# Loading x of seven of the 32 tiles in transfers of 120, 7 and 1 rows

## The chip, the cores and the metric

The kernel runs on one core of one Trainium2 chip. The metric is the device time of one execution in microseconds (us), taken as the median of several runs; each time comes from the chip itself. A profile of one execution, with the start and duration of every instruction and of every DMA packet, stands beside the times.

## The reference

The input x has 4096 rows of 32 fields with 64 numbers each; W has one 64x64 matrix for each of the 496 pairs of fields (i < j). For every row and pair, field i is multiplied by the pair's matrix, and the product is multiplied element by element by field j:

```python
vi = inputs[:, i_idx, :]                       # (B, 496, 64)
vj = inputs[:, j_idx, :]
vdotw = jnp.einsum('bpd,pde->bpe', vi, W)
inter = vdotw * vj
return inter.reshape(B, -1)                    # (4096, 31744), float32
```

x is 33.6 MB, W some 8 MB, the output 520 MB: nearly all that moves is the output.

## The kernel before

The 4096 rows are cut into 32 tiles t = 0..31 of 128 rows, one row to a partition. For each tile the kernel transposes x (TensorE, L130, two halves of eight 128x128 blocks, each copied out of PSUM by ScalarE at L131), multiplies by W (TensorE, L170), multiplies the result in PSUM by field j (VectorE, L180 and L188, written to the buffer `ring`), and stores `ring` to the output.

**Stores.** The 16 pairs of fields of a tile are grouped by `STORES` into four groups of 7552, 6528, 7872 and 9792 columns. Each group is stored by one DMA on SyncE's queue (L194), 128 rows of 30208, 26112, 31488 or 39168 bytes. `ring` has 28160 columns, fewer than the 31744 of one tile: a group's place is taken in turn, and starts again at 0 where the group no longer fits. VectorE may write a place only when the store that last read it has landed, so about three groups are on their way at a time. A DMA of 128 rows runs on all 16 DMA engines, 8 rows to each, and it has landed when the last of the 16 is done.

**Loads of x.** `xbuf` has three places for a tile of x, 2048 columns each. `x_slots` makes the list of loads: tile 0 alone, then two tiles to a load, `[(1,1),(2,2)]`, `[(4,0),(3,1)]`, `[(5,1),(6,2)]`, `[(8,0),(7,1)]` and so on (tile, place), and tile 31 alone. The host lays x out in this order, so that each partition's part of a load is one contiguous piece of DRAM, 16384 bytes for two tiles. `load_x` (L106) issues a load as one DMA on ScalarE's queue:

```python
nc.scalar.dma_start(
    out=xbuf[:, s * F * D : s * F * D + n],
    in_=x[at : at + P * n].rearrange("(p c) -> p c", p=P),
)
```

A load waits until VectorE has done the last product that reads the places it writes. For `[(8,0),(7,1)]` these are the places of tiles 4 and 5, so it goes out when tile 5 is done. The framework has eight semaphores for completions of DMAs and gives them out in turn; an issue also waits until the last DMA that had the semaphore has landed.

**Order on ScalarE's queue.** Between two loads stand four copies L131 (two tiles of two halves). The first half of tile t+1 is transposed at group member `FIRST_HALF_AT` = 9 of tile t, in the last of the four groups; its second half at member `SECOND_HALF_AT` = 3 of tile t+1 itself, in the second group.

**W** is loaded once at the start by five DMAs on SyncE's queue (L142).

Of the kernel before, what the change touches and what calls it, by code (L numbers as in the profile page):

```python
# [1 line left out]

# [6 lines left out]

F32 = mybir.dt.float32  # L10
ALU = mybir.AluOpType

P = 128
BANK = 512
BANKS = 8

STORES = [[0, 1], [2, 3], [4, 5, 6], [7, 8, 9, 10, 11, 12, 13, 14, 15]]

LOADS = [[0], [1], [2, 3], [4, 5, 6], [7, 8, 9, 10, 11, 12, 13, 14, 15]]


FIRST_HALF_AT, SECOND_HALF_AT = 9, 3
RING = 28160


def x_slots(NT):


    loads = [[(0, 0)]]
    for t in range(1, NT, 2):  # L30
        if t + 1 == NT:
            loads.append([(t, 1)])
        elif loads[-1][-1] == (t - 1, 2):
            loads.append([(t + 1, 0), (t, 1)])
        else:
            loads.append([(t, 1), (t + 1, 2)])
    return loads


@with_exitstack  # L40
def pair_bilinear_kernel(
    ctx: ExitStack,
    tc: tile.TileContext,
    x: bass.AP,
    w: bass.AP,
    out: bass.AP,
    F: int,
    D: int,
):

    nc = tc.nc
    NT = out.shape[1] * 2 // (F * (F - 1) * D)
    NPR = F // 2

    width = [(F - 1 - i) * D for i in range(F)]
    off = [sum(width[:i]) for i in range(F)]
    cols = sum(width)  # L80


    woff = [i % 2 * D + sum(width[i % 2 : i : 2]) for i in range(F)]
    store_w = [sum(width[2 * p] + width[2 * p + 1] for p in g) for g in STORES]

    const = ctx.enter_context(tc.tile_pool(name="const", bufs=1))
    psum = ctx.enter_context(tc.tile_pool(name="ps", bufs=1, space=bass.MemoryType.PSUM))

    ident = const.tile([P, P], F32, tag="ident", name="ident")
    make_identity(nc, ident)  # L90

    def runs(tl, a, b, n):

        ap = tl[:, a : a + n]
        return bass.AP(ap.tensor, ap.offset, [list(ap.ap[0]), [b - a, 2], list(ap.ap[1])])

    xbuf = const.tile([P, 3 * F * D], F32, tag="x", name="x")
    x_loads = x_slots(NT)
    slot = {t: xbuf[:, ts(s, F * D)] for load in x_loads for t, s in load}

    def load_x(load):

        at = sum(len(before) for before in x_loads[: x_loads.index(load)]) * P * F * D
        n = len(load) * F * D
        s = load[0][1]
        nc.scalar.dma_start(  # L106
            out=xbuf[:, s * F * D : s * F * D + n],
            in_=x[at : at + P * n].rearrange("(p c) -> p c", p=P),
        )

    pring = psum.tile([P, BANKS * BANK], F32, tag="pring", name="pring")
    bank = 0

    def take_banks(n):

        nonlocal bank
        if bank + n > BANKS:
            bank = 0
        got = pring[:, bank * BANK : (bank + n) * BANK]
        bank = (bank + n) % BANKS  # L120
        return got

    xT = const.tile([P, NPR * P], F32, tag="xT", name="xT")

    def transpose_x(xt, g):

        n = 2 * BANK // P
        pt = take_banks(2)
        for c in range(n):
            nc.tensor.transpose(pt[:, ts(c, P)], xt[:, ts(n * g + c, P)], ident)  # L130
        nc.scalar.copy(xT[:, ts(g, 2 * BANK)], pt)  # L131

    ring = const.tile([P, RING], F32, tag="ring", name="ring")
    at = 0

    load_x(x_loads[0])
    w_sb = const.tile([P, sum(width[0::2])], F32, tag="w", name="w")
    done = 0
    for g in LOADS:

        upto = woff[2 * g[-1]] + width[2 * g[-1]]
        nc.sync.dma_start(out=w_sb[:, done:upto], in_=w[:, done:upto])  # L142
        done = upto

    transpose_x(slot[0], 0)
    for t in range(NT):
        xt = slot[t]
        for load in x_loads:
            if min(load)[0] == t + 1:
                load_x(load)  # L150
        for s, group in enumerate(STORES):
            if at + store_w[s] > RING:
                at = 0
            osb = ring[:, at : at + store_w[s]]
            at += store_w[s]
            o0 = off[2 * group[0]]
            for p in group:
                if p == SECOND_HALF_AT:
                    transpose_x(xt, 1)
                if p == FIRST_HALF_AT and t + 1 < NT:  # L160
                    transpose_x(slot[t + 1], 0)
                first = (width[2 * p] - 1) % BANK + 1
                for c1 in range(first, width[2 * p] + 1, BANK):
                    n = first if c1 == first else BANK
                    c0 = c1 - n
                    odd = width[2 * p + 1] and c1 > D
                    pm = take_banks(2)
                    for h in range(1 + bool(odd)):
                        a = woff[2 * p + h] + c0 - h * D
                        nc.tensor.matmul(  # L170
                            pm[:, h * BANK : h * BANK + n],
                            xT[h * D : (h + 1) * D, ts(p, P)],
                            w_sb[h * D : (h + 1) * D, a : a + n],
                            start=True,
                            stop=True,
                        )
                    xj = xt[:, (2 * p + 1) * D + c0 : (2 * p + 1) * D + c1]
                    o = [off[2 * p + h] - o0 + c0 - h * D for h in range(2)]
                    if odd and (c0 or c1 < width[2 * p]):
                        nc.vector.tensor_tensor(  # L180
                            runs(osb, o[0], o[1], n),
                            runs(pm, 0, BANK, n),
                            bass.AP(xj.tensor, xj.offset, [xj.ap[0], [0, 2], xj.ap[1]]),
                            ALU.mult,
                        )
                    else:
                        for h in range(1 + bool(odd)):
                            nc.vector.tensor_tensor(  # L188
                                osb[:, o[h] + h * D : o[h] + n],
                                pm[:, h * (BANK + D) : h * BANK + n],  # L190
                                xj[:, h * D :],
                                ALU.mult,
                            )
            nc.sync.dma_start(  # L194
                out=out[:, t * cols + o0 : t * cols + o0 + store_w[s]], in_=osb
            )


# [30 lines left out]
```

## Time and profile before

| | |
|---|---|
| median of 6 runs | 1336.81 us (1336.66 to 1337.1) |
| the profiled execution: its own time | 1336.8 us |
| its span, first to last instruction | 1335.0 us |
| PE busy | 1161.0 us (87%) |
| DVE busy | 1182.9 us (89%) |
| ACT busy | 66.1 us (5%) |
| DMA | 562.87 MB, mean 422 GB/s |
| mean granted TensorE clock | 0.964 |

PE is TensorE's matmuls, DVE is VectorE, ACT is ScalarE, SP is SyncE; a name with q behind it is the engine's instruction queue. Busy shares are means over the whole span. "A <- B" in a list of waits says that A stood idle until B. Of the DMA packets the trace has the queue, the start, the duration and the size, but not the engine that moved them: q1 is the queue that SP issues to, q10 that of ACT, q8 and q14 carry instructions. One row of a transfer is one packet, and every engine's share of a DMA ends with a packet of 4 bytes, its step of the completion semaphore. The times of the 16 steps of each semaphore are in the trace too.

### The profile page before, as it was taken

To read this page: it belongs to the slowest core of one execution; us is meant where nothing else is said; L and a number is where in the kernel's file an instruction comes from. 1 tells how busy PE (TensorE), PEld (TensorE's weight loads), DVE (VectorE), ACT (ScalarE), POOL (GpSimd) and SP (SyncE) were. 2 spreads that over 40 slices of the span, in tenths; PEclk is the share of its full clock that TensorE was granted. 3 is DMA by queue.
4 is the path that set the end of the run, shared out by engine and by line. 5 is a ranking of instruction groups with operands and counts; after the bars stand their busy time and mean duration, and the time that the engine had idled before them with its cause. 6 is when DMAs were issued, how large, how long until landed. Compare 5 with 4: busy or idle time off the path is not lost.

```text
span 1335.0 us, 13080 instructions
## 1 busy us (share of the span) xinstructions
PE 1161.0 (87%) x5376; PEld 545.7 (41%) x5376; DVE 1182.9 (89%) x1376; ACT 66.1 (5%) x65; POOL 0.7 (0%) x6
## 2 busy tenths in 40 slices
PE   6998989989898898998989889798998979989893
PEld 3443334443344543443444444344443434353441
DVE  5998989989899898998989899898998989989894
ACT  0000000000000000000000000000000000000000
POOL 0000000000000000000000000000000000000000
PEclk9999999999899899999989999999999999989997
DMA  9999999999999999999999999999999999999998
GB/s 397 433 430 431 432 425 431 417 433 431 412 425 410 420 430 427 425 416 433 405 432 431 420 428 411 432 426 420 429 413 431 426 407 418 429 420 424 428 425 352
DMA packets 21659, 562.87 MB, mean 422 GB/s; under 512 B 2400, under 2 KB 2400, under 8 KB 2656
## 3 DMA queue, kind: packets, MB, share of 16 engines
q1 hardware_dynamic: 19152, 528.49, 92.8%
q10 hardware_dynamic: 2448, 33.56, 5.9%
q8 instruction: 42, 0.69, 0.2%
q14 instruction: 17, 0.14, 0.0%
HBM read 41.94 MB, written 520.09 MB: 421 GB/s over the span
## 4 chain that ended last, share of the span: by engine, by line
DMA 46%; DVE 37%; issue 8%; PE 7%; DVEq 0%; ACT 0%
DMA out_dram<-ring 45%; DVE ring L180 32%; PE pring L170 7%; DVE ring L188 5%; DMA x<-in_x_dram 1%; DVEq L180 0%; PE pring L130 0%; ACT xT L131 0%; DVEq L225 0%
## 5 line engine op out<-in xcount | busy, mean ns | idle before, releaser
L170 PE MATMUL pring<-w,xT 64*128 64x512 f32 (+4 forms) x4864 | 1098.8, 564 | 145.7 <-DVE ring L180 133.8
L180 DVE TENSOR_TENSOR ring<-pring,x 128x1024 f32<-128x1024 f32 (+3 forms) x1056 | 1103.6, 1105 | 133.0 <-DMA out_dram<-ring 103.0
L170 PEld LDWEIGHTS pring<-w,xT 64*128 64x128 f32 x4864 | 490.2, 191 | 711.7 <-DVE ring L180 532.0
L131 ACT COPY xT<-pring 128x1024 f32<-128x1024 f32 x64 | 64.8, 1012 | 1224.0 <-PE pring L130 1224.0
L188 DVE TENSOR_TENSOR ring<-pring,x 128x64 f32<-128x64 f32 (+3 forms) x320 | 97.3, 353 | 1.5 <-DMA out_dram<-ring 0.9
L130 PEld LDWEIGHTS pring<-ident,x 128*128 128x128 f32 x512 | 55.5, 142 | 57.8 <-DVE ring L180 49.1
L130 PE MATMUL pring<-ident,x 128*128 128x128 f32 x512 | 70.8, 282 | 8.7 <-DMA x<-in_x_dram 8.7
L131 ACT ACT_TABLE_LOAD x1 | 1.3, 1283 | 1.7 <-PEq L221 1.7
masks.py:199 POOL TENSOR_SCALAR_AFFINE_SELECT ident<-ident 128x128 f32<-128x128 f32 x1 | 0.3, 292 | 0.1
masks.py:197 POOL MEMSET ident<- 128x128 f32 x1 | 0.2, 204 | 0.3 <-POOLq L221 0.3
L221 POOL MEMSET const-bfloat16-1.0<- 128x1 bf16 x1 | 0.1, 101 | 0.0
L221 POOL MEMSET const-uint8-127<- 128x1 uint8 x1 | 0.1, 101 | 0.0
L221 POOL MEMSET const-float32-0.0<- 128x1 f32 x1 | 0.1, 98 | 0.2 <-issue 0.2
L221 POOL MEMSET const-float32-1.0<- 128x1 f32 x1 | 0.1, 98 | 0.0
## 6 DMA issues: line engine op xcount, KB each, us to landing
out_dram<-ring SPq DMA_DIRECT2D x32, 4896.0 KB, 17.7
out_dram<-ring SPq DMA_DIRECT2D x32, 3936.0 KB, 17.9
out_dram<-ring SPq DMA_DIRECT2D x32, 3776.0 KB, 18.0
out_dram<-ring SPq DMA_DIRECT2D x32, 3264.0 KB, 18.6
x<-in_x_dram ACTq DMA_DIRECT2D x15, 2048.0 KB, 20.4
w<-in_w_dram SPq DMA_DIRECT2D x1, 2592.0 KB, 28.3
x<-in_x_dram ACTq DMA_DIRECT2D x2, 1024.0 KB, 12.8
w<-in_w_dram SPq DMA_DIRECT2D x1, 2016.0 KB, 22.3
```

What stands on the lines that cost most here:

```text
L130: nc.tensor.transpose(pt[:, ts(c, P)], xt[:, ts(n * g + c, P)], ident)
L131: nc.scalar.copy(xT[:, ts(g, 2 * BANK)], pt)
L170: nc.tensor.matmul(pm[:, h * BANK : h * BANK + n], xT[h * D : (h + 1) * D, ts(p, P)], w_sb[h * D : (h + 1) * D, a : a + n], start=True, st ...
L180: nc.vector.tensor_tensor(runs(osb, o[0], o[1], n), runs(pm, 0, BANK, n), bass.AP(xj.tensor, xj.offset, [xj.ap[0], [0, 2], xj.ap[1]]), ALU ...
L188: nc.vector.tensor_tensor(osb[:, o[h] + h * D : o[h] + n], pm[:, h * (BANK + D) : h * BANK + n], xj[:, h * D :], ALU.mult,)
L221: nc = bacc.Bacc("TRN2", target_bir_lowering=False, num_devices=1)
```

## The change

Tiles 4, 8, 12, 16, 20, 24 and 28, each of them the first of the two tiles of its load, are loaded in three transfers by rows: 0 to 119, 120 to 126, and 127. The other tile of such a load (3, 7, ... 27) becomes a transfer of 128 rows of its own. So seven of the 17 loads turn from one DMA into four. All other loads, the layout of x in DRAM, the stores and the arithmetic stay.

```diff
+PART_LOADED = [4, 8, 12, 16, 20, 24, 28]
+ROWS = [slice(0, 120), slice(120, 127), slice(127, 128)]
...
-        nc.scalar.dma_start(
-            out=xbuf[:, s * F * D : s * F * D + n],
-            in_=x[at : at + P * n].rearrange("(p c) -> p c", p=P),
-        )
+        dst = xbuf[:, s * F * D : s * F * D + n]
+        src = x[at : at + P * n].rearrange("(p c) -> p c", p=P)
+        if not any(t in PART_LOADED for t, _ in load):
+            nc.scalar.dma_start(out=dst, in_=src)
+            return
+        for k, (t, _) in enumerate(load):
+            c = ts(k, F * D)
+            for r in ROWS if t in PART_LOADED else [slice(0, P)]:
+                nc.scalar.dma_start(out=dst[r, c], in_=src[r, c])
```

In the changed program the order of the instructions on TensorE, VectorE and SyncE is that of before. On ScalarE's queue the three transfers of tile 8 (and likewise of 4, 12, ...) stand two copies earlier than the load did, since they now need the place of tile 4 alone; the 128 rows of tile 7 stand where the load stood.

## The prediction

> **What bounds the kernel now.** I read the page's busy slices first, then the waits, then the list of DMA issues, and last the trace's packets and semaphore steps.
>
> ```profile
> PE 1161.0 (87%) x5376; PEld 545.7 (41%) x5376; DVE 1182.9 (89%) x1376; ACT 66.1 (5%) x65; POOL 0.7 (0%) x6
> ...
> DMA  9999999999999999999999999999999999999998
> ...
> DMA out_dram<-ring 45%; DVE ring L180 32%; PE pring L170 7%; DVE ring L188 5%; DMA x<-in_x_dram 1%; DVEq L180 0%; PE pring L130 0%; ACT xT L131 0%; DVEq L225 0%
> ```
>
> The 16 DMA engines are at 90% or more nearly throughout, and stores are the largest part of the chain that ended last. The waits say that VectorE is held by stores, not by its own work:
>
> ```profile
> DVE ring L180 <- DMA out_dram<-ring: 103.0, 43, 6.2
> DVE ring L180 <- PE pring L170: 19.0, 10, 13.7
> ```
>
> VectorE needs (1182.9 + 19 + the few us of smaller gaps) / 32, some 38 us a tile; a tile takes 41 (between two x loads, issued at 253.9 and 335.8 us, lie two tiles in 81.9 us). So VectorE has 3 us a tile to spare, and waits for places in `ring`.
>
> A place is free when the slowest of 16 engines is done, and the engines are not alike. The DMA view of the window 1329.9 to 1334 us:
>
> ```profile
> DMA  0000000800000000000000800000000000000000
> ...
> DMA packets 7, 0.08 MB, mean 19 GB/s; under 512 B 5, under 2 KB 5, under 8 KB 5
> ```
>
> Two packets of the last store (2 x 39168 bytes is 0.08 MB) start here, one after the other: one engine works alone until 1333.6, while most ended at 1329.9. Its packets can be followed back, since on one engine each packet starts 4 ns before the last one ends. From about 111 us on the engine that finishes last is always the same unbroken chain. Its 8 rows of the four stores take 9.09, 7.95, 9.61 and 11.88 us (tile 2), those of the others 8.92, 7.72, 9.30 and 11.56: 38.5 against 37.5 us a tile. Two tiles with the x rows (8 x 0.611 = 4.9) make 2 x 38.5 + 4.9 = 81.9 us, just the time between two loads. The slow engine sets the pace. The step of the last engine comes 0.23 us behind the 15th in the first loads, and mostly 1.5 to 4.5 us behind it in the stores after 130 us.
>
> What the other 15 lose by it: fewer than 16 engines have a packet of q1 or q10 under way for 239 engine-us between 60 and 1325 us; 42 stretches of about 0.9, 37 in all, are those where one engine carries a q8 packet, which leaves 202 / 15 = 13.5 us for each. With the end (54.6 / 15 = 3.6) they have 17.1 us to spare.
>
> **The change, part by part.** The profiled run is 1336.8 us, as the median; its last data packet ends at 1333.6. So the run is that end plus 3.2.
>
> *The highest engine.* A tile's 128 rows are 8 to an engine, 8 x 0.611 / 2 = 2.44 us in rows of 16384 bytes. It loses these and gets 1/16 of one row, 512 bytes. That size is not in the trace: it lies between a packet of 4 bytes (9 ns) and one of 7424 (281 ns); 7936 bytes took 300, 16128 took 602, a line through which gives 0.02 to 0.03 us, and I take 0.03. The companion tile's rows become 8192 bytes, 309 ns instead of 305.5: 8 x 3.5 ns, 0.03. Two steps of 9 ns: 0.02. Net -2.36 us, seven times -16.5 (with 281 ns: -14.8).
>
> *Engines 0 to 6.* If 120 rows go 8 each to 15 engines and 7 rows one each to seven, each of the seven gets a row of 309 ns more, and 0.03 + 0.03 + up to 0.04 for the same small parts: +0.41, seven times +2.9. *The others of the 15:* +0.1, +0.7.
>
> *The sum.* Highest engine: 1333.6 - 16.5 = 1317.1, if always busy; at 63 us, where tile 4's part now goes out, each engine has several us of stores queued (first landings come 14.2 us after issue, own work at most 11.6), so a lead of 2.4 us doesn't starve it. Engines 0 to 6: 1329.9 - 13.5 + 2.9 = 1319.3. The latter is more and is the bound. 42 q8 packets fall unevenly (16384 bytes, 0.61 us of work): one or two more than the mean on the worst engine add 0.5 to 1.2. I take 1319.8, and 1319.8 + 3.2 = **1323.0 us**, 13.8 less. Low end: the highest engine's sum, 1320.3, less 3 for slowness that may lessen (below): 1317. High end of this case: a third of the idle time stays, +4.5: 1327.5.
>
> *The issues.* 21 more DMAs on ScalarE's queue at 0.365 us each (median of L106), 7.7 us in all, but three in a row at most. Behind them stands the copy of the next second half; at 335.8 us such a load is issued and the next copy starts at 346.6, so 10 us of idle time cover 1.1. Without that cover TensorE would wait 1.1 us seven times, and VectorE's 3 us a tile would take it. *The semaphores given out in turn:* the new issues wait for DMAs of at least a tile earlier: the single row of tile 8 for the load of 5 and 6, issued a tile before; SyncE's last store of tile 5 for the 120 rows of tile 8, also issued a tile before. A tile is 41 us, and the longest landing is 23.1. Nothing. *The earlier place:* the three parts of tile 8 go out when tile 4 is done, the companion when tile 5 is. The same bytes go through the same queues, in pieces of 2.4 instead of 4.9 us; the store that shares a load's time lands at 22 instead of 17 us, so two smaller delays take the place of one: nothing to half an idle stretch gained.
>
> [...] The rows: 256 packets of 8192 bytes took 309 ns and 1920 of 16384 bytes 611, so halving the piece costs 1% on the engine. [...]
>
> **The rivals.**
>
> *The slow engine isn't the relieved one* (no change). The packets carry no engine's number, so that the chain is the highest engine is not shown. If it is one of 7 to 14, 1333.6 + 0.7 + 3.2 = 1337.5; if one of 0 to 6, 1339.7. For it: nothing in the profile names it. Against it: the extra time that it has to lose, 17.1, is of the size of the relief, which says only that the relief could work. [...] The trace speaks for one slow chain: the second to end does so at 1331.1, only 1.2 us behind the rest.
>
> *The slowness follows whoever trails* (half the gain). The slow chain isn't slow in tiles 0 and 1 (9.30 us for the third store, as all), nor for some 15 us after each x load. Why is not to be read. If being last is what slows, another engine becomes last when this one is relieved. Between nothing and 13.8 I take half, 1330; for it stand the fast early tiles, against it that engines thrown back by a q8 packet (0.4 us and more) go on at full speed.
>
> *The pieces don't spread* (slower). The trace before shows only 128 rows over 16 engines. If 120 rows go to 8 engines, 15 each, these get 7 x 7 x 0.309 = 15.1 us more, and if 7 rows go to one engine, that one 15.1 again: 1329.9 - 13.5 + 30.3 + 0.7 + 3.2 = 1350.6. With the 7 rows alone on one engine it is 1335.4. It decides from 17.1 us more on any one engine; below that there is still a gain. [...]
>
> **How the numbers follow.** A measurement of this kernel tells about 0.2%, 2.7 us, from no change. Forecast (1317 to 1327.5): 0.72. Slowness follows (1327.5 to 1334): 0.11. Not the relieved engine: 0.09, of which 0.05 within 0.2% and 0.04 above it. Pieces don't spread: 0.06, of which 0.02 within 0.2% and 0.04 above. A residue of 0.02 for an unseen wait, slower. So faster 0.83, same 0.07, slower 0.10. The range 1317 to 1333 holds the first two cases, 0.82.
>
> **What would show it.** Right: the two tiles between loads take some 81 us instead of 81.9 on average; VectorE's wait for stores falls from 103 us to below 60; the last step of 16 comes within 2.5 us of the 15th; packets of 512 bytes take 0.02 to 0.05 us, and no engine carries more than 8 rows of a part. Wrong: one chain still trails by 3 us and more in every store (not the relieved engine), rows of 8192 bytes come 15 to an engine (no spread), or waits of ScalarE or SyncE for a DMA appear.

## The result, and the profile after

The changed kernel takes 1340.34 us (median of 15 runs, 1339.89 to 1340.72), the kernel before 1336.85 in the same comparison: slower by 3.5 us, ratio 1.0026 with an interval of 1.0019 to 1.0033. The forecast was 1323.0. The rival "the slow engine isn't the relieved one" gave 1339.7 for a slow engine among 0 to 6.

The page of the changed kernel, queues and span:

```profile
span 1338.4 us, 13133 instructions
...
q1 hardware_dynamic: 19152, 528.49, 92.6%
q10 hardware_dynamic: 3505, 33.56, 5.9%
q8 instruction: 42, 0.69, 0.2%
```

q10 had 2448 packets before. Of the 3505 now, 2048 have 8192 bytes, 1024 have 16384 and 433 are steps of 4 bytes. Of the steps, 17 transfers of 128 rows account for 17 x 16 = 272; the other 161 are 7 x 23, and 23 = 15 + 7 + 1. So 120 rows did go to 15 engines and 7 to seven, but the single row went to one engine as a packet of 8192 bytes; there is no packet of 512.

The waits of VectorE in the changed kernel, beside 103.0 and 19.0 before:

```profile
DVE ring L190 <- DMA out_dram<-ring: 107.3, 44, 6.2
DVE ring L190 <- PE pring L180: 18.1, 8, 13.6
```

The wait for stores was to fall below 60 us; it grew by 4.3. And the end of the changed kernel, its DMA view from 1333.2 to 1338 us:

```profile
DMA  0000007000000000007000000000000000000000
...
DMA packets 6, 0.08 MB, mean 16 GB/s; under 512 B 4, under 2 KB 4, under 8 KB 4
```

This is the picture of before, 3.2 us later: two rows of the last store, one after the other, on one engine alone (to 1336.8; before, to 1333.6). One chain of packets, each starting as the last one ends, still trails the others. Its cycle can be read in the packets as the time between the ends of the second stores of tiles 0, 4, 8 ... 28. These seven periods are longer than before by 0.36 to 0.71 us, 0.46 on average and 3.2 in all: each has one part-loaded tile in it, and one row of 8192 bytes is 0.31 us. So the slow engine seems not to have been relieved but to have got a row more; the runs below test this.

### The profile page after: what moved, and what is told of

Its sections match the earlier page's. It is cut to its first block, busy times and chain, and to the rows that moved or that the text cites. A ratio compares the mean times of both kernels' runs of the same rounds, so it can differ in the third digit from the quotient of the medians.

```text
span 1338.4 us, 13133 instructions
## 1 busy us (share of the span) xinstructions
PE 1159.4 (87%) x5376; PEld 542.6 (41%) x5376; DVE 1182.4 (88%) x1376; ACT 66.1 (5%) x65; POOL 0.7 (0%) x6
## 3 DMA queue, kind: packets, MB, share of 16 engines
q10 hardware_dynamic: 3505, 33.56, 5.9%
## 4 chain that ended last, share of the span: by engine, by line
DMA 47%; DVE 37%; issue 9%; PE 5%; DVEq 0%; ACT 0%
DMA out_dram<-ring 46%; DVE ring L190 32%; DVE ring L198 6%; PE pring L180 5%; DMA x<-in_x_dram 1%; DVEq L190 0%; PE pring L140 0%; ACT xT L141 0%; DVEq L235 0%; DVEq L198 0%
```

## The experiments

Theory A: one fixed engine, among the low-numbered ones, is slow, and its own bytes set the time. Theory B: whoever trails is slowed. Theory C: the order and the issues of the new transfers cost, not the shares of the engines. The median of the kernel before was 1336.9 us in every comparison.

**The split alone, with all shares equal** (e1). Against the changed kernel:

```diff
-ROWS = [slice(0, 120), slice(120, 127), slice(127, 128)]
+ROWS = [slice(0, 128)]
```

> Seven loads are cut into two transfers of 128 rows, one a tile, with the early place of the change, but every engine keeps its 8 rows of each tile. Fixed slow engine among the low-numbered ones (theory A): the extra row of the change is gone, only shorter rows and steps remain, 1337.0 to 1337.6 us. Whoever trails is slowed (theory B): the same, 1337. Cost of order and issues, not of shares (theory C): as the change, 1340.

1337.47 us (1337.36 to 1337.57). The early place, the shorter rows and the seven extra issues cost 0.6 us. Theory C expected 1340 here and falls; the other 2.9 us come with the cut into 120, 7 and 1 rows, that is with the shares and with two more transfers a tile (e3 tells these apart).

**A code by engine** (e2). The last 8 rows are cut differently in the seven tiles:

```diff
-ROWS = [slice(0, 120), slice(120, 127), slice(127, 128)]
+CUT = {4: 127, 8: 127, 12: 126, 16: 126, 20: 125, 24: 125, 28: 124}
...
-            for r in ROWS if t in PART_LOADED else [slice(0, P)]:
+            for r in [slice(0, 120), slice(120, CUT[t]), slice(CUT[t], P)] if t in PART_LOADED else [slice(0, P)]:
```

> As the change with three transfers a tile, but the last 8 rows are cut 7+1, 7+1, 6+2, 6+2, 5+3, 5+3 and 4+4 over the seven tiles, so that engines 0 to 7 get 14, 12, 10, 8, 6, 4, 2 and 0 rows more than with 120 rows (if a transfer of n rows under 16 goes one each to the n lowest engines), each 0.309 us. Theory A: the time above the kernel of e1 tells the number of the slow engine: engine 0 +4.3, 1 +3.7, 2 +3.1, 3 +2.5, 4 +1.9, 5 +1.2, 6 +0.6. Theory B: the engine with most sets it, +4.3. Theory C: 1340, as the change.

1340.21 us, 2.74 over e1. By the expected sums that would be engine 3 (2.5) or 2 (3.1). The periods of the slow chain tell it tile by tile; over those of e1 they are longer by

| last 8 rows cut | 7+1 | 7+1 | 6+2 | 6+2 | 5+3 | 5+3 | 4+4 |
|---|---|---|---|---|---|---|---|
| us more than e1 | 0.49 | 0.50 | 0.40 | 0.58 | 0.32 | 0.31 | 0.04 |

So the slow engine has a row in the transfers of 7, 6 and 5 rows and none in those of 4, 3, 2 or 1: if n rows go to the n lowest engines, it is number 4, the fifth. (This is what "engine 4" means from here on, and "engines 0 to 3" are the four that come before it in this count; no packet shows a number.) Its six rows are 1.9 us; 0.5 more comes with the third transfer of a tile, as the next run shows, and some 0.4 isn't accounted for.

**Two transfers of 4 rows** (e3).

```diff
-ROWS = [slice(0, 120), slice(120, 127), slice(127, 128)]
+ROWS = [slice(0, 120), slice(120, 124), slice(124, 128)]
```

> As the change, but the last 8 rows go in two transfers of 4: engines 0 to 3 get two rows more a tile, 14 in all, 4.3 us, engines 4 to 14 none. Theory A: about 4.3 us over e1 if the slow engine is one of 0 to 3, about 0 to 0.3 if it is 4 to 6. Theory B: +4.3. Theory C: 1340.

1337.93 us (1337.62 to 1338.3), 0.46 over e1. This run says three things. If the two transfers of 4 rows go to the same four engines in every tile, these took 14 rows more each, 4.3 us, and the time did not follow them, though theory B as put above expected +4.3. (At 0.6 us a part-loaded tile they need not have come to trail; e5 and e7 show the case in which they do.) The 15 engines that carry 120 rows keep 8 each, and the one left over, the prediction's "highest", has none: taking 7 x 8 rows of 0.31 us from it, 17 us of work if it is the same one each time, is worth nothing. And the difference to the change, 120, 7 and 1 rows at 1340.34, is 2.4 us, seven rows of 0.31 (2.2) on an engine that a transfer of 7 rows reaches and one of 4 does not.

**The output laid out by tiles** (e4).

```diff
-                out=out[:, t * cols + o0 : t * cols + o0 + store_w[s]], in_=osb
+                out=out[t * P : (t + 1) * P, o0 : o0 + store_w[s]], in_=osb
...
```

> The kernel before, with the output in DRAM laid out tile by tile (a row of a store lies 126976 bytes behind the last instead of 4063232; the host only puts the rows back in order). If the slow engine is slow for the addresses it writes (theory D), the pace changes: up to 17 us faster, 1320, or another engine becomes slow. If it is the engine itself, 1337.

1336.71 us, ratio 0.9999 (0.9990 to 1.0007). The distance between the rows that the stores write doesn't make the slow engine.

**Relief for engine 4, in three tiles** (e5).

```diff
-PART_LOADED = [4, 8, 12, 16, 20, 24, 28]
-ROWS = [slice(0, 120), slice(120, 127), slice(127, 128)]
+PART_LOADED = [8, 16, 24]
+ROWS = [slice(0, 68), slice(68, 128)]
```

> Tiles 8, 16 and 24 are loaded in transfers of 68 and 60 rows. If 68 rows go 17 each to engines 0 to 3 and 60 rows 4 each to engines 0 to 14, engine 4 has 4 rows instead of 8, engines 0 to 3 have 21. Theory A, the slow one is engine 4: it loses 3 x 4 x 0.309 = 3.7 us, engines 0 to 3 gain 12.1, less than the 17.1 that they have to spare; 1333.5, some 3.4 under the kernel before. If the slow one is among 0 to 3: +12, 1349. If the load of an engine does not count at all (theory C): 1337.3.

1338.35 us, and unsteady (1336.47 to 1340.08). The steps in the packets are 3 x 19 above 272, so 68 rows went to 4 engines and 60 to 15, as meant. The periods without a part-loaded tile are about as long as before or shorter (162.2, 164.5, 163.7, 162.5 us; before 162.4, 164.3, 163.8, 164.4), but two of the three with one have 166.3 and 166.1 instead of 163.8: engines 0 to 3 get 4 us of work at once, and that puts them behind the slow one. The forecast of 1333.5 missed this.

This settles theory B. At the second store of tile 24 the engine that ends last takes 7.72 us for its 8 rows of 26112 bytes, the usual time, while an engine that ends 2.8 us before it takes 7.95, as the trailing one did in the kernel before. So the engine that trails isn't slowed by trailing, and the slow one stays slow when it doesn't trail.

**The same in two tiles, further apart** (e12).

```diff
-PART_LOADED = [4, 8, 12, 16, 20, 24, 28]
-ROWS = [slice(0, 120), slice(120, 127), slice(127, 128)]
+PART_LOADED = [8, 20]
+ROWS = [slice(0, 68), slice(68, 128)]
```

> Tiles 8 and 20 alone in transfers of 68 and 60 rows: engine 4 loses 8 rows, 2.5 us, engines 0 to 3 gain 26, 8.0 us, with twelve tiles between the two. Theory A with engines 0 to 3 making up 4 us in ten tiles, as the others' idle time of 13.5 us in 30 tiles allows: 1335. If the 4 us cannot be made up: 1338, as with three tiles.

1334.86 us (1334.66 to 1336.74) against 1336.93, ratio 0.9987, interval 0.9978 to 0.9996: the only one of the kernels with all their work whose interval lies below 1. The span and the queue of the x loads, from its page:

```profile
span 1333.0 us, 13090 instructions
...
q10 hardware_dynamic: 2742, 33.56, 5.9%
```

Of the 2742 packets, 2432 are rows (1664 of 16384 bytes and 768 of 8192), and 310 are steps, 272 + 2 x 19: each tile went to 4 + 15 engines, as meant. Engine 4 loses four rows of 0.31 us in each of the two tiles, 2.5 us, and the span is 2.0 shorter than the 1335.0 of before. At the end the slow engine is the second to last, 0.2 us before another.

**In five tiles** (e7). Against e5:

```diff
-PART_LOADED = [8, 16, 24]
+PART_LOADED = [4, 8, 16, 20, 24]
```

> As 68 and 60 rows in three tiles, but in five (4, 8, 16, 20, 24): engine 4 loses 6.2 us, engines 0 to 3 gain 5 x 13 x 0.309 = 20.1, more than the 17.1 to spare. By the sum of the prediction engines 0 to 3 then set the end: 1329.9 - 13.5 + 20.1 + 0.5 + 3.2 = 1340. If the spare time were much more than 17, 1331.

1344.08 us (1343.0 to 1345.55), beyond the 1340 of the sum. So the 17.1 us "to spare" are no pot to draw from at will. They come at 13.5 us in some 30 tiles, less than half a us a tile. Before, most engines end a store some 4 us ahead of the slow one; here an engine that gets 4 us more at once ends behind it (at the second store of tile 24, by 3.7 us, again at the usual 7.72 us for 8 rows), and the others wait for that one.

**Load on engine 4** (e6).

```diff
-PART_LOADED = [4, 8, 12, 16, 20, 24, 28]
-ROWS = [slice(0, 120), slice(120, 127), slice(127, 128)]
+PART_LOADED = [8, 16, 24]
+ROWS = [slice(0, 115), slice(115, 128)]
```

> The same three tiles in transfers of 115 and 13 rows: if 115 rows go 23 each to engines 0 to 4 and 13 rows one each to 0 to 12, engine 4 has 24 rows instead of 8, 48 more in all, 14.8 us. Theory A: 1352. If the slow one is 5 or higher: it loses 7 rows a tile, 6.5 us, and engines 0 to 4 keep within 17.1: 1332 to 1335. Theory C: 1337.3.

1352.25 us (1351.8 to 1352.78), ratio 1.0115 (1.0101 to 1.0129), as theory A has it. The steps are 3 x 18 above 272, so 115 rows went to five engines. Five engines instead of four, in the same three tiles, turn +1.4 into +15.3 us, though not by the fifth engine alone: here each of the five has 24 rows, in e5 each of the four 21.

**GpSimd's queue** (e9). In the seven part-loaded tiles, instead of `ROWS` (and 5 rows of tile 0 and 11 of tile 31 by GpSimd, the rest of them by ScalarE):

```diff
+            nc.gpsimd.dma_start(out=dst[0:120, c], in_=src[0:120, c])
+            nc.gpsimd.dma_start(out=dst[120:121, c], in_=src[120:121, c])
+            nc.scalar.dma_start(out=dst[121:125, c], in_=src[121:125, c])
+            nc.scalar.dma_start(out=dst[125:128, c], in_=src[125:128, c])
```

> In seven tiles 120 rows and 1 row are loaded from GpSimd's queue, 4 and 3 rows from ScalarE's; tile 0 gives GpSimd's queue 5 rows first. If that queue hands its transfers of 120 and 1 rows to 15 engines and 1 engine in turn, beginning behind the five of tile 0, engine 4 gets one row a tile instead of 8 and engines 0 to 3 two or three more: theory A then gives up to 7 x 7 x 0.309 = 15 us less, bounded by the other engines' spare time, 1322 to 1330. If it hands them always to the same 15 engines, 0 to 14, it is as e3: 1337 to 1339. If engine shares don't matter: 1337.

1344.08 us (1343.8 to 1344.78). The seven periods are 2.2 us longer in all than in e1, so engine 4 got no relief; 5 us more are lost outside them, mostly at the start, where the three transfers of tile 0 land later (VectorE's wait for TensorE is 26.1 instead of 19.0 us). Whether these transfers went to engines 0 to 14 or to others isn't to be read from it.

**What makes the engine slow.** Of the next five kernels, each in one profiled run, four leave work out; f2 leaves out none. First the stores alone: transposes, products and multiplications are gone, and `ring` is filled once (e8).

```diff
-    transpose_x(slot[0], 0)
+    nc.vector.memset(ring, 0.0)
...
-            for p in group:
-                ...
```

> The transposes, the matrix products and the products with field j are left out: ring is filled with zeros once, and w, x and all stores go out with no wait for VectorE. If engine 4 is slow by itself, one engine ends some 20 to 30 us after the other 15, which end near 1316. If it is slowed by the work of the other engines on the memories, all 16 end together within 3 us.

1328.11 us, and no engine trails. The DMA view of the last 2 us, 1324 to 1326.3: 

```profile
DMA packets 16, 0.00 MB, mean 0 GB/s; under 512 B 16, under 2 KB 16, under 8 KB 16
```

Only the 16 steps remain; they come within 0.5 us. Next, VectorE fills `ring` with copies of x, so that it waits for stores as in the kernel (e10), or multiplies what stands in PSUM, with all its instructions (e11). In e10, with the loop over p and the transposes gone:

```diff
+            for c in range(0, store_w[s], 1024):
+                nc.vector.tensor_copy(osb[:, c : min(c + 1024, store_w[s])], slot[t][:, : min(1024, store_w[s] - c)])
```

In e11, where the calls of `transpose_x` are gone too:

```diff
+    nc.vector.memset(pring, 1.0)
...
-                        nc.tensor.matmul(
-                            pm[:, h * BANK : h * BANK + n],
-                            ...
-                        )
```

> Transposes, matrix products and the products with field j are left out; VectorE fills each group of ring by copies of x, so that stores are released by VectorE and VectorE waits for stores as in the kernel, without TensorE, ScalarE copies or PSUM. If the slow engine comes from the waiting for the last of 16 engines, one engine trails as in the kernel, 1330 to 1337. If it comes from TensorE's or PSUM's traffic or from the instruction packets, all engines end together, 1310 to 1325.

> Transposes, copies and matrix products are left out; VectorE multiplies what stands in PSUM by field j, with all its instructions as in the kernel. If TensorE's work (or its instruction packets) slows the one engine, it ends with the others, near 1320; if not, the trailing chain and 1337 stay.

1322.69 us with the 16 engines together again; and 1326.5 us with four engines 2 to 4 us behind at the end, but at the pace of the others (their 8 rows of 31488 bytes mostly take the usual 9.30 us). So the waiting for the last of 16 doesn't by itself slow one engine. What the three have in common is that TensorE does nothing, that ScalarE copies nothing and that q8 is gone. The queues of e11:

```profile
q1 hardware_dynamic: 19152, 528.49, 93.5%
q10 hardware_dynamic: 2448, 33.56, 5.9%
q14 instruction: 13, 0.11, 0.0%
```

The line of q8, 42 packets in the changed kernel as before, is missing. The last two kernels tell the columns that TensorE multiplies from its instructions. f1 keeps every instruction at L170 but cuts the product to one column; f2 cuts each product of more than 256 columns in two. Both keep a load of 64x128 weights (PEld) with every product.

```diff
+    nc.vector.memset(pring, 1.0)
...
-                            pm[:, h * BANK : h * BANK + n],
+                            pm[:, h * BANK : h * BANK + 1],
...
-                            w_sb[h * D : (h + 1) * D, a : a + n],
+                            w_sb[h * D : (h + 1) * D, a : a + 1],
```

```diff
+                        for m0 in range(0, n, 256):
+                            m = min(256, n - m0)
...
+                                pm[:, h * BANK + m0 : h * BANK + m0 + m],
```

> Every matrix product of L170 is cut to one column (PSUM is filled once and VectorE multiplies what stands there), so TensorE keeps its instructions, their packets on q8 and all waits, but nearly none of its work. If the slow engine comes from the instructions of TensorE, one chain trails by 2 to 4 us as in the kernel, 1333 to 1337. If it comes from TensorE's work (reads of x and w, writes of PSUM), there is none, near 1326 as without TensorE.

> Every matrix product of more than 256 columns is cut in two, the work the same and the instructions of TensorE nearly doubled. If the slow engine comes from instructions, its extra of about 1 us a tile grows towards 2 us, and the time by some 20 to 30 us, 1355 to 1365. If it comes from the work, 1337 to 1340.

f1 takes 1336.65 us, as the kernel before (1336.91 beside it), and one chain trails as there. TensorE's busy times, and the end from 1329.7 to 1334 us:

```profile
PE 829.3 (62%) x5376; PEld 736.6 (55%) x5376; DVE 1181.5 (89%) x1377; ACT 66.1 (5%) x65; POOL 0.7 (0%) x6
```

```profile
DMA  0000000800000000000008000000000000000000
...
DMA packets 10, 0.08 MB, mean 18 GB/s; under 512 B 8, under 2 KB 8, under 8 KB 8
```

Two slices with bytes in them, 1.5 us apart, are the two last rows, one engine working alone; the other engines are done. So with one column instead of up to 512, but all of TensorE's instructions and weight loads, one engine is still slow (8 rows of 31488 bytes in 9.58 to 9.61 us). TensorE's products are busy 829 us instead of 1161, far from nothing.

f2 takes 1355.33 us. TensorE's busy times, the queue of the instructions, and below them the waits of VectorE:

```profile
PE 1180.2 (87%) x9472; PEld 975.3 (72%) x9472; DVE 1184.3 (88%) x1376; ACT 66.1 (5%) x65; POOL 0.7 (0%) x6
...
q8 instruction: 74, 1.21, 0.3%
```

```profile
DVE ring L182 <- DMA out_dram<-ring: 115.0, 44, 6.7
DVE ring L182 <- PE pring L172: 22.8, 17, 13.5
```

q8 has 74 packets instead of 42, 32 more, and the time is 18.4 us longer: 0.58 us for each. The longer time is mostly not TensorE's own: VectorE waits for it 22.8 us, against 19.0 before, but for stores 115 against 103. The slow rows are slower still: the four stores of tile 16 take the trailing engine 9.19, 8.06, 9.80 and 12.08 us, 39.13 in all, where before they took 38.53. These 0.60 us a tile, over 32 tiles, are about the 18.4.

So what slows the one engine grows with the number of TensorE's instructions and hardly with the columns they multiply. f1 and f2 are one run each, and neither parts the instructions from their weight loads: f2 has 9472 of both instead of 5376, and f1 keeps all. Which of the two it is, no run shows; nor whether the q8 packets, which are the instructions' only visible load on the DMA engines, have to do with it.

## Why the prediction was wrong, point by point

**What bounds the kernel: right.** One engine sets the pace. Where its bytes grow, the time moves by about as much: some 0.3 us a row in the change and in e2, +15.3 in e6 (14.8 reckoned). Where they shrink, it gains (-2.1 in e12) until other engines fall behind it (e5, e7).

**The step that failed** is "the highest engine: 1333.6 - 16.5". The profile showed one slow chain, and the prediction took it for the highest engine, because the change relieves that one and the sizes matched (17.1 to spare, 16.5 relieved), which proved to be chance. No packet carries a number, as the text itself said; the 0.09 given to the rival was too little. e3 puts the worth of that relief at nothing: with no x rows of seven tiles on the engine left over, the time is 0.46 us above e1. The term that counted was the next one, "engines 0 to 6, +0.41 a tile, +2.9": put on the slow chain it gives 1333.6 + 2.9 + 3.2 = 1339.7, and 1340.34 was measured. That the sum comes so near owes something to luck: its 2.9 holds 0.7 of small parts that were estimates. By the runs, of the 3.5 us 0.6 come with the split at equal shares (e1), 0.5 with the further transfers (e3), and 2.4 with the rows of 120, 7 and 1, where seven rows of 0.31 make 2.2.

**Small terms.** No run shows the size of the relief, since it fell on an engine that didn't bind. The single row was reckoned as 16 pieces of 512 bytes, 1/16 of it on the relieved engine, which no run of a load from ScalarE's queue shows: in the changed kernel it was one packet of 8192 on one engine. It isn't the slow one, so this moved nothing. That 120 rows go to 15 engines and 7 to seven was a condition of the sum; the steps of the changed kernel agree, 7 x (15 + 7 + 1). That the seven are engines 0 to 6 and the one left out by the 120 rows is the highest, no run shows, since no packet carries a number; e2, e3 and e6 fit a count from the lowest engine up throughout, with engine 4 the slow one.

**The order, the issues, the semaphores:** 0.6 us with seven more transfers (e1) and 1.0 with 21 (e3), where nothing was reckoned. Small, as forecast.

**"The slowness follows whoever trails"** is refuted by e5 and e7, where engines that trail run at the usual pace (7.72 us for 8 rows of 26112 bytes); in e5 another stays slow (7.95). The slow engine is one that a transfer of 5 rows reaches and one of 4 does not (e2).

**"The pieces don't spread"** didn't happen.

**The 17.1 us to spare** were wrong as a budget that can be drawn in bursts: e5 asks for 12.1 us of them and e7 for 20.1, 4 us at a time, and both lose. Whether the total holds for small even parts, no run shows. So even had the slow engine been relieved, the 13.8 us were not shown to be there for the taking; the 7 tiles of the change would have given each other engine 0.1 to 0.4 us at a time, which no run tried with the slow engine free.

**Left open:** whether TensorE's instructions or the weight loads that come with them burden engine 4, and by what way. The q8 packets themselves stretch rows of other engines too (by about 0.4 us each), while the trailing engine's rows are all a little longer, 20 to 50 ns each. Nor is it settled why its rows are at full speed before about 111 us (in f2, to 78 us) and for some 15 us after an x load. In the last store, from 1322 us on, when TensorE and VectorE are done, the trailing engine's 8 rows take 11.56 us as everyone's, against 11.88 in tile 16; this fits a cause in the engines' work but doesn't say in which.

## What to carry to other kernels

A trailing chain in the packets says that one of 16 engines is slow, not which one: number it before spending work on it. Cutting a few rows into transfers of n rows, n differing from tile to tile, and reading the period of the chain tile by tile does so in one run, if it is known which engines a transfer of n rows takes. Where all engines have the same bytes and one trails, look for what else loads it, and spread any bytes moved to the others over time: here their spare time came to less than half a us a tile, and 4 us at once in three or five of 32 tiles lost 1.4 and 7.2 us (e5, e7).

## What the runs showed of the hardware

- With TensorE's instructions in the program, one DMA engine moved its rows about 3% slower (9.6 instead of 9.30 us for 8 rows of 31488 bytes in the kernel before) from some 111 us on. With 32 more instruction packets of 16384 bytes (f2) the time was 18.4 us longer, 0.58 us for each; with TensorE and ScalarE's copies left out, the kernels took 1322.7 to 1328.1 us, and no single engine trailed at a slower pace.
- One column instead of up to 512 in every product (TensorE busy 829 instead of 1161 us) changed the time by 0.3 us; cutting products in two, with the same columns in all but nearly twice the instructions and weight loads, by 18.4.
- The slow engine was slow also where it didn't trail: 7.95 us for 8 rows of 26112 bytes at the second store of tile 24 in e5, while the last engine took 7.72.
- A transfer of a single row of 8192 bytes from ScalarE's queue went to one engine (one packet and one step in each of the seven tiles of the changed kernel); from GpSimd's queue, in e9, it came as 16 packets of 512 bytes (112 in seven tiles, 27 ns each).
